# Which engine copies which turn of the probabilities: even turns to ScalarE and odd ones to VectorE, exponents dealt behind turns 0 and 4, batch 8 loaded in two parts (Flamingo block, two layers, one core)

## The chip, the core and the metric

The kernel runs on one core of a Trainium2 chip. The metric is the device time in microseconds (us) of a whole execution; lower is better. Engines are called as in the profile: PE (TensorE), PEld (its weight loads), DVE (VectorE), ACT (ScalarE), POOL (GpSimd), SP (SyncE). Besides times of several runs there is one execution recorded by the hardware profiler, whose rows are called the trace here.

## The reference

Two gated layers on a residual stream x of 8 batches of 100 rows of 512. Each layer is a cross attention over a context of 722 rows (16 heads of 32) and then a feed-forward network. Layer 0 masks the context and its network is ternary; layer 1 has an output projection and a network with quantised activations and weights.

```python
# x (8, 100, 512), ctx (8, 722, 512), mask (8, 722), 16 heads of 32
x = x + tanh(g_xattn[0]) * xattn0(layernorm(x), ctx, ctx, mask)
x = x + tanh(g_ffn[0])   * ffn0(layernorm(x))
x = x + tanh(g_xattn[1]) * xattn1(layernorm(x), ctx, ctx)
x = x + tanh(g_ffn[1])   * ffn1(layernorm(x))

def xattn(x_q, x_k, x_v):               # q, k, v: projections with biases, split into heads
    scores = einsum('bhqw,bhkw->bhqk', q, k) / sqrt(32)
    scores = scores - 10000.0 * (1.0 - mask)      # layer 0 alone
    p = softmax(scores, axis=-1)
    h = einsum('bhqk,bhkw->bhqw', p, v)
    return h                            # layer 1: h @ Wo.T + bo
```

## The kernel before, in words

Everything is one stream of instructions, whose order is written out by hand: each engine runs its instructions in the order in which the program issues them, and waits on semaphores where it needs another engine's result. The program holds the whole computation twice, and the second copy runs only where a test of the inputs asks for it; in the runs here one copy runs.

`attention` goes through 8 batches b and, in each, 4 groups oc of 4 heads. One group is: `scores` of the first half of the keys (L387: 4 matmuls, L395; DVE adds the bias and takes the maximum, L404), a loop of 5 steps, `scores` of the second half, `exponents` started with `negm` (L418, DVE, the negated row maximum), `between`, and `settle`. What is settled is the group before, so probabilities are turned one group after their scores. The four exponents of a group (`next(exps)`, L421, ACT, 0.90 us each) are issued during the `settle` of the group before it and, what is left of them, in the loop of the next group.

`settle` (L506) has six turns, c = 0 to 5, called t0 to t5 here. A `turn` (L430) is 4 transposes of 120 or so keys into a PSUM bank (L436) and one copy of that bank to SBUF, by DVE (L439) or by ACT (L441); `vector` is true wherever both take part: in layer 0 and for b = 0 to 6 of layer 1. For b = 7 of layer 1 ACT copies all of them. The tag `pst` has two banks, so the transposes of t2 need the copy of t0 to be done, t3 that of t1, and so on; other tiles use the same two banks (`ps_xn` of the layernorm, the rows of `finish`, the quantised rows). After each turn follow, in this order: `take(0.74)`, which issues so many us of fill; an exponent, if c is in `dealt`; and a step of `state["spare"]`. Fill is the next batch's projections of keys and values (`projections`, L263): matmuls into one of two other banks and their evictions (layer 0: kT by ACT L321, v by DVE L341 and L342; layer 1, in three passes: kT by ACT L285 and then DVE L288, v by ACT L301 and then DVE L302). After the six turns `values` (L444) multiplies all six copies, in the order of the turns, by v (L448) into a part of the bank of t4, and DVE copies the result (L455).

Around this stand other pieces of DVE work, in the order of the program. `finish` (L457) closes a batch; its chain is issued during oc = 0 and oc = 1 of the next batch (layer 0: L468 to L498 and L135; layer 1: L481, L487, L496, L498, L135). `between0` issues, for oc = 1 in layer 0, `mask_bias` of the next batch (three DVE operations on 100x722, L991, L993, L994), ahead of the settle's turns; for (b, oc) = (6, 3) it starts `normalised`, a layernorm (L142 to L163), and for later groups splits of it (L584, L585). `between1` sets `state["spare"]` to the quantisation of token rows (L820 to L845, with `ln_rstd`, L155 to L159, and L163) for some groups with oc = 0 and oc = 2 of b = 4 to 7.

The context is loaded in parts by `PARTS`: in layer 0 two of 384 and 338 columns, in layer 1 three of 242, 240 and 240. Layer 1 works with a three-pass split (`make_split`), but its first batch, called batch 8 here, is projected during layer 0's last batch by the plain `make`: for each part, 4 x 4 matmuls into `ps_k` (L313) and 4 evictions to kT. `load_ctx(B, 2)` in `follow0` (L1025) loads its third part.

Of the kernel before, what the change touches and what calls it, by code (L numbers as in the profile page):

```python
# [9 lines left out]
F32 = mybir.dt.float32  # L10
F32R = mybir.dt.float32r
# [11 lines left out]
B, S, D = 8, 100, 512  # L23
# [3 lines left out]
P = 128  # L27
KC = D // P
# [2 lines left out]
HALF = SK // 2  # L31
NK = 6

PARTS = ([(0, 384), (384, 338)], [(0, 242), (242, 240), (482, 240)])
KEYS = (
    [(c * P, min(P, SK - c * P)) for c in range(NK)],
    [(0, 122)] + [(122 + c * 120, 120) for c in range(NK - 1)],
# [16 lines left out]
def flow(tc: tile.TileContext, a: dict, out: bass.AP, verdict):  # L54
# [23 lines left out]
    rooms = {}  # L78
# [37 lines left out]
    def take(us):  # L116
        state["owed"] += us * state["pace"]
        while state["owed"] > 0:
            spent = next(state["fill"], None)
            if spent is None:  # L120
                state["owed"] = 0.0
                return
            state["owed"] -= spent
# [64 lines left out]
    def load_ctx(i, part):  # L188
        k0, kn = PARTS[i // B][part]
        t = rooms["ctx"].tile([P, KC, PARTS[0][0][1]], F32, tag="ctxT", name=f"ctxT{i}_{part}")  # L190
        nc.sync.dma_start(t[:, :, :kn], a["ctxT"][i % B][:, :, k0 : k0 + kn])
        ctx_tiles[i, part] = t

    def split_ctx(i, part, idle=False):


        k0, kn = PARTS[1][part]
        sets = [
            rooms["ctx"].tile([P, KC, PARTS[1][0][1]], F32R, tag=t, name=t, bufs=2)
            for t in ("ctx_h", "ctx_l", "ctx_d")  # L200
        ]
        engine = nc.vector if idle else nc.gpsimd
        for half in range(2):
            cs = slice(half * KC // 2, (half + 1) * KC // 2)
            raw = rooms["ctx"].tile([P, KC // 2, PARTS[1][0][1]], F32, tag="ctx_raw", name="ctx_raw")
            nc.sync.dma_start(raw[:, :, :kn], a["ctxT"][i % B][:, cs, k0 : k0 + kn])
            xh, xl, xd = (t[:, cs, :kn] for t in sets)
            if idle:
                nc.scalar.activation(xh, raw[:, :, :kn], AF.Copy, scale=HIGH)
            else:  # L210
                nc.gpsimd.tensor_scalar_mul(xh, raw[:, :, :kn], HIGH)  # L211
            engine.tensor_sub(xl, raw[:, :, :kn], xh.bitcast(F32))
            if idle:
                nc.scalar.activation(xl, xl.bitcast(F32), AF.Copy, scale=LEAP)
            else:
                nc.gpsimd.tensor_scalar_mul(xl, xl.bitcast(F32), LEAP)
            engine.tensor_sub(xd, xh.bitcast(F32), xl.bitcast(F32))
        ctx_tiles[i, part] = sets
# [27 lines left out]
    def three_passes(ps, n, xs, ws, key_cols, out_cols, keys_move):  # L246


        for col, which in ((0, (0, 1)), (256, (2,))):
            for c in range(KC):  # L250
                for k in which:
                    x, w = xs[k][:, c, key_cols], ws[k][:, c, out_cols]
                    nc.tensor.matmul(  # L253
                        ps[:, col : col + n],
                        w if keys_move else x,
                        x if keys_move else w,
                        start=(c == 0 and k == which[0]),
                        stop=(c == KC - 1 and k == which[-1]),
                    )
                    if (col, c) != (256, KC - 1):  # L260
                        yield n / 2400 + 0.016

    def projections(i, wk, wv, bk, more):  # L263
# [3 lines left out]
        layer = i // B  # L267
# [3 lines left out]
            load_ctx(i + 1, 0)  # L271

        def make_split():
            for part, (k0, kn) in enumerate(PARTS[1]):
                xs = ctx_tiles.pop((i, part))
                if part < 2:
                    split_ctx(i, part + 1)
                elif more:
                    split_ctx(i + 1, 0)
                for oc in range(KC):  # L280
                    ps = ps_p.tile([P, 512], F32, tag="ps", name="ps_k")
                    rows_of = slice(oc * P, (oc + 1) * P)
                    yield from three_passes(ps, kn, xs, wk, slice(0, kn), rows_of, True)
                    dst = kT[:, oc, k0 : k0 + kn]
                    nc.scalar.activation(  # L285
                        dst, ps[:, :kn], AF.Identity, scale=1.0 + 1.0 / LEAP, bias=bk[:, oc : oc + 1]
                    )
                    nc.vector.scalar_tensor_tensor(  # L288
                        dst, ps[:, 256 : 256 + kn], -1.0 / LEAP, dst, ALU.mult, ALU.add
                    )  # L290
                    yield kn / 2400 + 0.016
                for half in range(2):
                    cols = slice(half * 256, (half + 1) * 256)
                    for kc, (r0, rn) in enumerate(KEYS[1]):
                        if not k0 <= r0 < k0 + kn:
                            continue
                        ps = ps_p.tile([P, 512], F32, tag="ps", name="ps_v")
                        keys = slice(r0 - k0, r0 - k0 + rn)
                        yield from three_passes(ps[:rn], 256, xs, wv, keys, cols, False)
                        dst = v[half][:rn, kc, :]  # L300
                        nc.scalar.activation(dst, ps[:rn, :256], AF.Copy, scale=1.0 + 1.0 / LEAP)  # L301
                        nc.vector.scalar_tensor_tensor(  # L302
                            dst, ps[:rn, 256:], -1.0 / LEAP, dst, ALU.mult, ALU.add
                        )
                        yield 256 / 2400 + 0.016
# [77 lines left out]
    def attention(layer, kv, follow, qT, bias_of, between, wo, bv, bo, pick):  # L383
# [46 lines left out]
        def turn(ps, c, vector):  # L430

            k0, kn = KEYS[layer][c]
            bank = ps_t.tile([P, 512], F32, tag="pst", name="ps_pT")
            pt = bank[:, : 4 * S].rearrange("p (j s) -> p j s", j=4)
            for j in range(4):
                nc.tensor.transpose(pt[:kn, j, :], ps[j][:, k0 : k0 + kn], ident[:S, :S])  # L436
            sb = rooms["pT"].tile([P, 4, S], F32, tag="pT", name="pT", bufs=6)
            if vector and c % 2 == 0:
                nc.vector.tensor_copy(sb[:kn], pt[:kn])  # L439
            else:  # L440
                nc.scalar.copy(sb[:kn], pt[:kn])  # L441
            return sb, bank[:, 4 * S : 5 * S]

        def values(oc, v, pT, o, oT):  # L444
            for c, (k0, kn) in enumerate(KEYS[layer]):
                for j in range(4):
                    cols = slice((4 * oc % 8 + j) * W, (4 * oc % 8 + j + 1) * W)
                    nc.tensor.matmul(  # L448
                        o[j * W : (j + 1) * W, :],
                        v[oc // 2][:kn, c, cols],  # L450
                        pT[c][:kn, j, :],
                        start=(c == 0),
                        stop=(c == NK - 1),
                    )
            nc.vector.tensor_copy(oT[:, oc, :], o)  # L455
# [50 lines left out]
        def settle():  # L506
            b0, oc0, v0, ps0, oT0, sums0 = held
            vector = layer == 0 or b0 < B - 1
            dealt = (1, 4) if layer and 0 < b0 < B - 1 else (0, 2, 4)
            got = []  # L510
            for c in range(NK):
                got.append(turn(ps0, c, vector))
                take(0.74)
                if c in dealt:
                    next(exps, None)
                next(state["spare"], None)
            values(oc0, v0, [g[0] for g in got], got[NK - 2][1], oT0)
            if oc0 < KC - 1:
                return iter(())
            end = finish(b0, oT0, sums0)  # L520
            next(end)
            return end
# [38 lines left out]
        def last():  # L561
            for _ in exps:
                yield
            take(1.5)
            for _ in settle():
                yield
# [455 lines left out]
    def follow0(b):  # L1022
        if b + 1 < B:
            return projections(b + 1, wk, wv, bk, True)
        load_ctx(B, 2)  # L1025
        later["kv"] = projections(B, wk1, later["wv"], bk1, False)
        return later["kv"]

# [2 lines left out]
    def between0(b, oc):  # L1031
# [8 lines left out]
        if (b, oc) >= (B - 2, KC - 1):  # L1040
            later["xs"] = next(entering)

    ending = attention(0, kv, follow0, qT, lambda b: biases[b], between0, None, bv, None, None)
    for _ in inspected:
        pass
# [286 lines left out]
```

## Time and profile before

| what | value |
|---|---|
| median of 3 runs | 1822.77 us (1818.52 to 1824.11) |
| profiled execution | 1816.73 us, its span 1814.8 us |
| mean granted clock of TensorE | 0.976 |
| layer 0's attention, about | 45 to 605 us |
| layer 0's network, about | 605 to 1165 us |
| layer 1's attention, about | 1215 to 1627 us, its last batch and the rows' network to the end |

Times in the trace are us from the start of the span. In the groups of the page the number behind the bar is busy time and the mean of one instruction in ns, and behind the second bar the idle time of the engine just before them, with the releaser that ended most of it. In the list of waits the numbers are us in total, times, and the longest. A line of the timeline has the start, the duration, the engine, the source line, the operation with its tiles, how many of them, and in brackets the idle time before it and what ended that.

### The profile page before, as it was taken

How to read it: one execution, taken by the hardware profiler on the slowest of the kernel's cores; microseconds unless marked ns; L12 is line 12 of the kernel's file. 1: busy time of each engine (PE TensorE's matmuls, PEld its weight loads, DVE VectorE, ACT ScalarE, POOL GpSimd, SP SyncE). 2: the span in 40 equal slices, each digit the busy share in tenths (PEclk: the TensorE clock that was granted, in tenths of full speed). 3: DMA queues.
4: the chain of work that ended last, by engine and by line, in shares of the span. 5: the costliest groups of instructions: out<-in, count | busy, mean ns of one | idle time of the engine just before them, and what ended most of it. 6: DMA issues, size and time to landing. Idle time of an engine off the chain costs nothing. (4 is left out here: it accounts for less than half of the span.)

```text
span 1814.8 us, 30628 instructions
## 1 busy us (share of the span) xinstructions
PE 1698.7 (94%) x12491; PEld 1308.2 (72%) x12491; DVE 871.9 (48%) x2412; ACT 641.9 (35%) x1349; POOL 666.6 (37%) x543
## 2 busy tenths in 40 slices
PE   8999999999989999999989999899999999998876
PEld 4555555555555899999988999878888877874443
DVE  2545555545555421145451011445555666767764
ACT  1133333333334444422231111234444544453431
POOL 0798998882030000010000000224555444513222
PEclk9999999999999999999999999999999999999888
DMA  7345444451130368778674555410011000110000
GB/s 205 121 146 160 142 156 152 142 167 40 29 117 1 119 222 291 263 251 301 225 231 141 183 186 181 148 45 24 23 28 29 23 23 24 29 71 5 6 10 21
DMA packets 64332, 212.33 MB, mean 117 GB/s; under 512 B 7426, under 2 KB 30978, under 8 KB 51822
## 3 DMA queue, kind: packets, MB, share of 16 engines
q0 software_dynamic: 25344, 138.42, 23.5%
q1 hardware_dynamic: 38838, 71.86, 13.0%
q8 instruction: 100, 1.64, 0.4%
q14 instruction: 50, 0.41, 0.1%
HBM read 205.48 MB, written 4.78 MB: 116 GB/s over the span
## 5 line engine op out<-in xcount | busy, mean ns | idle before, releaser
L604 PE MATMUL ps_h<-hi,h 128*128 128x400 f32 x1024 | 359.4, 351 | 0.0
L604 PE MATMUL ps_h<-lo,h 128*128 128x400 f32 x1024 | 357.1, 349 | 0.0
L421 ACT ACTIVATE p<-p,negm 100x722 f32<-100x722 f32 x256 | 229.3, 897 | 117.9 <-DVE negm L418 117.6
L436 PEld LDWEIGHTS ps_pT<-ident,p 100*128 100x128 f32 (+3 forms) x1536 | 164.9, 139 | 118.3 <-issue 41.0
L436 PE MATMUL ps_pT<-ident,p 100*128 100x100 f32 (+3 forms) x1536 | 199.6, 253 | 32.0 <-DVE pT L439 17.3
L333 PE MATMUL ps_v<-wv,ctxT 128*128 128x512 f32 (+3 forms) x432 | 217.9, 615 | 0.0
L313 PE MATMUL ps_k<-ctxT,wk 128*128 128x384 f32 (+3 forms) x608 | 204.1, 465 | 8.7 <-DMA ctxT<-in_ctxT 8.7
L731 POOL TENSOR_TENSOR seen<-seen,part 128x1024 int32<-128x1024 int32 x88 | 209.2, 2377 | 7.5
L585 DVE TENSOR_TENSOR lo<-g,hi 128x400 fp32r<-128x400 f32 x96 | 55.2, 575 | 305.9 <-ACT hi L584 305.9
L604 PEld LDWEIGHTS ps_h<-lo,h 128*128 128x128 f32 x1024 | 195.7, 191 | 0.5
L604 PEld LDWEIGHTS ps_h<-hi,h 128*128 128x128 f32 x1024 | 195.7, 191 | 0.5
L579 POOL DMA_DIRECT2D h<-in_h_w x64 | 34.7, 541 | 376.5 <-PE ps_h L604 368.6
L439 DVE COPY pT<-ps_pT 128x400 f32<-128x400 f32 (+1 forms) x180 | 102.9, 571 | 114.7 <-PE ps_pT L436 113.7
L313 PEld LDWEIGHTS ps_k<-ctxT,wk 128*128 128x128 f32 x608 | 107.2, 192 | 63.5 <-issue 29.0
L404 DVE CUSTOM_DVE_ANT_0 p<-sc,mask 100x361 f32<-100x361 f32 x256 | 121.3, 531 | 62.0 <-PE sc L395 61.6
L441 ACT COPY pT<-ps_pT 120x400 f32<-120x400 f32 (+3 forms) x204 | 99.6, 490 | 101.7 <-PE ps_pT L436 99.6
L211 POOL TENSOR_SCALAR ctx_h<-ctx_raw 128x480 fp32r<-128x480 f32 (+1 forms) x40 | 56.7, 1417 | 214.5 <-PE ps_v L253 164.0
L404 DVE CUSTOM_DVE_ANT_0 p<-sc,zero 100x361 f32<-100x361 f32 x256 | 121.7, 531 | 24.8 <-PE sc L395 24.4
L659 ACT ACTIVATE g<-ps_h,h_s 128x400 f32<-128x400 f32 x64 | 38.1, 596 | 243.5 <-PE ps_h L604 243.5
L333 PEld LDWEIGHTS ps_v<-wv,ctxT 128*128 128x128 f32 (+3 forms) x432 | 70.7, 187 | 54.6 <-issue 52.9
L321 ACT ACTIVATE kT<-ps_k,bk 128x384 f32<-128x384 f32 (+3 forms) x76 | 41.6, 547 | 181.9 <-PE ps_k L313 181.1
L730 POOL CAST part<-w_seen 128x1024 int32<-128x1024 uint16 x88 | 92.4, 1050 | 27.2 <-DMA w_seen<-in_h_w 17.9
(199 smaller groups left out, 3028.1 us busy)
## 6 DMA issues: line engine op xcount, KB each, us to landing
h<-in_h_w POOLq DMA_DIRECT2D x64, 1024.0 KB, 5.3
w_seen<-in_h_w POOLq DMA_DIRECT2D x64, 512.0 KB, 4.1
w<-in_w POOLq DMA_DIRECT2D x16, 1024.0 KB, 5.3
w_seen<-in_w POOLq DMA_DIRECT2D x16, 512.0 KB, 4.1
w_gate<-in_w_gate SPq DMA_DIRECT2D x16, 512.0 KB
w_up<-in_w_up SPq DMA_DIRECT2D x16, 512.0 KB
w_down<-in_w_down SPq DMA_DIRECT2D x16, 512.0 KB
w<-in_w_w POOLq DMA_DIRECT2D x8, 1024.0 KB, 6.4
```

Of the source, the lines that this page charges most:

```text
L211: nc.gpsimd.tensor_scalar_mul(xh, raw[:, :, :kn], HIGH)
L313: nc.tensor.matmul(ps[:, :kn], wk[:, c, oc * P : (oc + 1) * P], cT[:, c, :kn], start=(c == 0), stop=(c == KC - 1),)
L333: nc.tensor.matmul(ps[:rn, :], cT[:, c, r0 - k0 : r0 - k0 + rn], wv[:, c, :], start=(c == 0), stop=(c == KC - 1),)
L404: nc.vector.tensor_tensor_reduce(ps[j][:, cols], sc[j][:S, :HALF], bias[:, cols], 1.0, LOWEST, ALU.add, ALU.max, m2[:, j, h : h + 1],)
L421: nc.scalar.activation(ps[j], ps[j], AF.Exp, bias=negm[:, j : j + 1], accum_out=sums[:, 4 * oc + j : 4 * oc + j + 1],)
L436: nc.tensor.transpose(pt[:kn, j, :], ps[j][:, k0 : k0 + kn], ident[:S, :S])
L439: nc.vector.tensor_copy(sb[:kn], pt[:kn])
L441: nc.scalar.copy(sb[:kn], pt[:kn])
L585: nc.vector.tensor_sub(two[1][:, cols], src, two[0][:, cols].bitcast(F32))
L604: nc.tensor.matmul(acc[:, :TH], w[:, c, :], part, start=(c == 0 and k == 0), stop=(c == len(ins) - 1 and k == len(two) - 1),)
L730: nc.gpsimd.tensor_copy(part, low)
L731: nc.gpsimd.tensor_tensor(seen, seen, part, ALU.add)
```

## The change

1. In `turn`, where `vector` holds, ACT copies t0, t2 and t4 and DVE copies t1, t3 and t5; before it was the other way round.
2. In `settle`, exponents are dealt behind t0 and t4 wherever `vector` holds. Before, layer 1 with 0 < b0 < 7 dealt them behind t1 and t4, and all the rest behind t0, t2 and t4; b0 = 7 of layer 1 stays so. The exponents not dealt are issued in the loop of the next group.
3. Batch 8 is loaded and projected in two parts, of 362 and 360 columns; the splits of batches 9 to 15 keep their three parts under the new name `SPLIT_PARTS`, and `load_ctx(B, 2)` goes.

```diff
-PARTS = ([(0, 384), (384, 338)], [(0, 242), (242, 240), (482, 240)])
+PARTS = ([(0, 384), (384, 338)], [(0, 362), (362, 360)])
+SPLIT_PARTS = [(0, 242), (242, 240), (482, 240)]
...
     def split_ctx(i, part, idle=False):
-        k0, kn = PARTS[1][part]
+        k0, kn = SPLIT_PARTS[part]
...
         def make_split():
-            for part, (k0, kn) in enumerate(PARTS[1]):
+            for part, (k0, kn) in enumerate(SPLIT_PARTS):
...
         def turn(ps, c, vector):
...
-            if vector and c % 2 == 0:
+            if vector and c % 2:
                 nc.vector.tensor_copy(sb[:kn], pt[:kn])
             else:
                 nc.scalar.copy(sb[:kn], pt[:kn])
...
         def settle():
...
             vector = layer == 0 or b0 < B - 1
-            dealt = (1, 4) if layer and 0 < b0 < B - 1 else (0, 2, 4)
+            dealt = (0, 4) if vector else (0, 2, 4)
...
     def follow0(b):
         if b + 1 < B:
             return projections(b + 1, wk, wv, bk, True)
-        load_ctx(B, 2)
         later["kv"] = projections(B, wk1, later["wv"], bk1, False)
```

Lines are those of the kernel before; in the changed kernel they are one higher from `split_ctx` on.

More of the change, by code (lines that the diff above doesn't have):

```diff
@@ L194, in split_ctx @@
     def split_ctx(i, part, idle=False):
-        k0, kn = PARTS[1][part]
+        k0, kn = SPLIT_PARTS[part]
         sets = [
-            rooms["ctx"].tile([P, KC, PARTS[1][0][1]], F32R, tag=t, name=t, bufs=2)
+            rooms["ctx"].tile([P, KC, SPLIT_PARTS[0][1]], F32R, tag=t, name=t, bufs=2)
             for t in ("ctx_h", "ctx_l", "ctx_d")
@@ L204, in split_ctx @@
             cs = slice(half * KC // 2, (half + 1) * KC // 2)
-            raw = rooms["ctx"].tile([P, KC // 2, PARTS[1][0][1]], F32, tag="ctx_raw", name="ctx_raw")
+            raw = rooms["ctx"].tile([P, KC // 2, SPLIT_PARTS[0][1]], F32, tag="ctx_raw", name="ctx_raw")
             nc.sync.dma_start(raw[:, :, :kn], a["ctxT"][i % B][:, cs, k0 : k0 + kn])
```

## The prediction

> **What bounds the kernel now.** The page first. TensorE (PE) is busy 1698.7 of 1814.8 us, and only 32.0 us of its idle time stand before the transposes of the probabilities, the step that this change touches:
>
> ```profile
> PE 1698.7 (94%) x12491; PEld 1308.2 (72%) x12491; DVE 871.9 (48%) x2412; ACT 641.9 (35%) x1349; POOL 666.6 (37%) x543
> ...
> L436 PE MATMUL ps_pT<-ident,p 100*128 100x100 f32 (+3 forms) x1536 | 199.6, 253 | 32.0 <-DVE pT L439 17.3
> ...
> L439 DVE COPY pT<-ps_pT 128x400 f32<-128x400 f32 (+1 forms) x180 | 102.9, 571 | 114.7 <-PE ps_pT L436 113.7
> ```
>
> DVE and ACT have room; a copy costs about the same on both (571 and 490 ns), so the change can win only by when a copy is done. The waits of PE say which copies are late:
>
> ```profile
> PE ps_pT L436 <- DVE pT L439: 17.3, 14, 5.4
> PE ps_pT L436 <- ACT pT L441: 11.2, 9, 2.6
> ...
> PE ps_pT L448 <- ACT pT L441: 2.3, 6, 0.4
> PE ps_pT L448 <- DVE pT L439: 2.2, 5, 1.2
> ```
>
> That is 33 us, the pool from which it is paid. Third, the timeline at these waits, which have two places. In layer 1, groups with oc = 1:
>
> ```profile
> 1280.57 0.13 DVE L418 TENSOR_REDUCE negm<-m 100x4 f32<-100x8 f32 x1
> 1280.61 0.56 DVE L439 COPY pT<-ps_pT 122x400 f32<-122x400 f32 x1
> 1280.73 0.90 ACT L421 ACTIVATE p<-p,negm 100x722 f32<-100x722 f32 x1 [0.61 <-DVE negm L418]
> ...
> 1281.23 0.56 PE L436 MATMUL ps_pT<-ident,p 100*120 100x100 f32 x4 [1.00 <-DVE pT L439]
> ```
>
> The chain of `finish` has kept DVE until 1280.6; turn 0's copy (call turns t0 to t5) comes behind it and `negm`; t2 needs t0's bank and waits 1.00. In layer 0, oc = 1, `mask_bias` stands ahead of the copies instead:
>
> ```profile
> 295.64 0.47 ACT L441 COPY pT<-ps_pT 128x400 f32<-128x400 f32 x1
> 296.17 0.57 PE L436 MATMUL ps_pT<-ident,p 100*128 100x100 f32 x4 [1.80 <-ACT pT L441]
> 296.26 1.63 DVE L994 TENSOR_SCALAR mask<-mask,mask_m 100x722 f32<-100x722 f32 x1
> 297.81 0.56 DVE L439 COPY pT<-ps_pT 128x400 f32<-128x400 f32 x1
> 298.43 0.56 PE L436 MATMUL ps_pT<-ident,p 100*128 100x100 f32 x4 [0.81 <-DVE pT L439]
> ```
>
> t1 was copied first, by ACT, but behind an exponent that waits for `negm`; t2 took its bank and t3 that of t0. Last, the granted clock by windows behind two such waits (PE column, then the clock, third from the end):
>
> ```profile
> 165.80:169.20 3.40, 3.36 (x11) 2.22 (x12) 1.13 (x3) 1.38 (x3) 3.32 (x3) 0.52 0.48 154
> 298.40:301.80 3.40, 3.37 (x18) 2.00 (x18) 1.70 (x4) 1.64 (x4) 3.31 (x3) 1.00 0.46 154
> ```
>
> After PE waited 1.93 us it ran at 0.52 for some 3.4 us, which costs 1.7; after 1.80 it did not.
>
> **Part 1, the copies, layer 0.** After the change t0 goes to ACT at once, ahead of the first exponent, so t2 starts on time; t1's copy takes on DVE the place that t0's had, and t3 waits for it. What counts is when t3 starts.
> - b = 1, 3, 4 (before: waits of .55 + 1.93, 1.80 + .81, 2.37 + .82): t3 starts at the same moment as now. Gain 0. The two waits become one of 2.4 to 3.2 us. At b = 1 and 4 the clock fell already; at b = 3 it did not, and by the rows (1.93, 2.37 and 2.58 dropped it) it will: -1.7.
> - b = 2: t2's wait of 2.58 ended at 230.81 and its fill ran at half clock, so that t3 began at 233.28; DVE's copy ends at 231.85. Gain 1.0 to 1.4, taken 1.0.
> - b = 0: wait .36 goes; t3 would start at 96.0, DVE's copy ends at 95.07. Gain .36. b = 5, 6: t2's .43 goes, t3 then waits some .2: gain .2 each.
> - b = 6, oc = 3, where `normalised` holds DVE: one wait of 5.38 until 525.74. t2 and its fill (1.2 us) now run inside the wait. Gain 1.2 to 1.9, taken 1.5.
> - Three waits of 1.1 on L585 concern t1's bank, which another tile holds: unchanged.
> Sum 0.4 + 1.0 + 0.4 + 1.5 - 1.7 = 1.6; bounds -0.5 (t3's copy a little late everywhere) and 4.5 (no drop, the larger ends).
> [...]
>
> **Part 1, layer 1, b < 7.**
> - oc = 1, b = 1 to 6: waits of t2 of 1.00 (three) and 1.15 (three), 6.45 in all. After: DVE's copy, now of t1, ends at 1281.17, and t3, with t2 on time at 1280.23, is due at 1281.2. t4 needs t2's copy on ACT, behind an exponent: 1280.73 + .90 + .49 = 1282.1, due 1282.2. The later three leave .15 each: gain 6.0.
> - oc = 3, b = 1 to 6: `values` stops .39 each time in its last part, since t5's copy on ACT stands behind the exponent dealt behind turn 4:
>
> ```profile
> 1312.64 0.90 ACT L421 ACTIVATE p<-p,negm 100x722 f32<-100x722 f32 x1
> 1313.52 0.48 ACT L441 COPY pT<-ps_pT 120x400 f32<-120x400 f32 x1
> 1314.05 0.38 PE L448 MATMUL ps_pT<-pT,v 120*32 120x100 f32 x8 [0.39 <-ACT pT L441]
> ```
>
> t5's copy is now DVE's, behind L302 (1312.78 + .42), done by 1313.8 where 1313.66 would be on time: .1 to .15 stays. Of 2.34, 1.4 to 2.3 gained, taken 1.8.
> - Groups with token rows on DVE (oc = 2 of b = 4, 5, 6): t0's copy escapes the chain L155 to L163, t1's does not (it moves from ACT to behind L155 to L159, .67 mean to .88, .16, .16, .25), so that t3 waits, and t5's lands behind L836 or L839. Each 0.4 to 0.6 worse, taken 1.5 for the three.
> - b = 0, oc = 3: .67 + .32 stay but for .1. Settle of (6,3), during b = 7: the 1.16 before `values` on t4 at 1646.17 is put off to t5, whose matmuls start 1.0 later, but t3 waits in between: 0 to 1, taken .4.
> Sum 6.0 + 1.8 - 1.5 + .1 + .4 = 6.8; bounds 4 and 8.5.
>
> **Part 2, the exponents.** Layer 0 (and b = 0 of layer 1): the one behind turn 2 goes to the next group's loop, so ACT has two there instead of one; layer 1: one moves from behind turn 1 to turn 0. Two take 2 x .90 us of a loop of over 6, and the turns that read them come a loop later; the kT evictions (L321, .58) that may queue behind them have a second bank and four matmuls (2.8 us) of slack. Cost nothing; without that cover .9 a group, which no row shows. Behind turn 0 or 1 the exponent waits for `negm` alike, and no copy of t0 waits behind it any more.
>
> **Part 3, batch 8.** 48 matmuls of 240 columns become 32 of 360. In the timeline of L313 one of 240 takes .45 us, of 338 .61, of 384 .69; so .65 for 360: 48 x .45 - 32 x .65 = 0.8 us on PE, which is the bound there (562 to 592). Bounds 0 and 1.5. Four evictions and one load fewer were hidden; SP issues one DMA less ahead of the scales.
>
> **Sum.** 1.6 + 6.8 + 0.8 = 9.2 us of the profiled execution's 1816.73: 0.51%. That execution lies 0.33% under the median 1822.77; the same share of the median gives 1813.5.
>
> **Rivals.**
> - *No clock drop at b = 3*: 1.7 better, 1811.8. For: the 1.80 there dropped nothing, and neither did three waits of 1.1.
> - *The wait only moves*: in oc = 1 of layer 1, t3 waits for t1's DVE copy as t2 did for t0's, as in layer 0. The 6.0 go and 3.2 stay: 1819.6, within 0.3% (5.5 us, about what a measurement here can tell from no change). For: the copy ends at 1281.17 against a due time of 1281.2, no slack at all. Against: a .1 late costs only .1.
> - *Slower: t5 on DVE comes last.* DVE evicts values in pairs (L302 with L288, .42 + .41; L341 with L342, pitch .33), and each settle's last copy now stands behind them and right before `values`, which reads it 1.07 us after it begins. With .57 for the copy, .5 is spare; from a DVE backlog over .5 us on, each of some 46 settles that have no wait at their end now loses .4 (one eviction): 46 x .4 = 18.4, less 9.2, is 9.2 slower, 1832. For: the page has DVE 50 to 70% busy in the slices of layer 1. Against: t4's copy had to be done sooner, and for it `values` waited only 5 times, 2.2 us.
>
> **How the numbers follow.** Forecast (with the drop) .58, without it .12: together faster by over 0.3%, .70. Moved wait, or half of it with the token rows worse: same, .16. Slower: .14, .12 of it the third rival. The terms' bounds give 3.5 to 14.5 us, 1808 to 1819; the moved wait reaches 1819.6, part of the third rival 1824, and the before's runs spread from 1818.5 to 1824.1, so the range is 1806 to 1824.
>
> **What would show it.** The waits of L436 on DVE and ACT together fall from 28.5 to some 20, on DVE alone hardly in layer 0 (its rows stand at t3 now), in layer 1 from 8.0 to under 3; L448 on ACT loses its six of .39, L448 on DVE grows a little. L313 has 16 x 2 records fewer. The window behind 298.4 shows a clock near .5. Wrong: L448 waits on DVE in most settles (third rival), t3 waits near 1.0 in oc = 1 of layer 1 (second), or waits of `ps_k` on L321 in layer 0.

## The result, and the profile after

The changed kernel took 1815.5 us in the median of 10 runs (1808.93 to 1816.88), the kernel before 1823.44 in 10 (1816.96 to 1828.67): a ratio of 0.9963, 95% interval 0.9946 to 0.9980. Measured again later beside other kernels, it had 0.9980 (0.996 to 1.000; 12 runs). So it is faster by 0.2 to 0.4%, 4 to 7 us; forecast were 9.2 us, 0.51%.

The two profiled executions do not show this gain: 1816.86 us after, near the slowest run of its ten, against 1816.73 before, below the fastest of its ten. Totals of single traces are therefore not compared below; stages are, over several traces. Page of the changed kernel:

```profile
PE 1701.9 (94%) x12459; PEld 1302.0 (72%) x12459; DVE 875.5 (48%) x2412; ACT 641.0 (35%) x1345; POOL 666.1 (37%) x543
...
L437 PE MATMUL ps_pT<-ident,p 100*128 100x100 f32 (+3 forms) x1536 | 199.6, 253 | 31.9 <-DVE pT L440 24.0
```

The idle time of PE before the turns' transposes is what it was, 31.9 against 32.0 us. Its releasers have changed, as the list of waits of PE shows (us in total, times, longest):

```profile
PE ps_pT L437 <- DVE pT L440: 24.0, 16, 4.8
...
PE ps_pT L437 <- DVE xc L586: 4.5, 4, 1.4
PE ps_pT L437 <- ACT pT L442: 3.0, 3, 1.2
...
PE ps_pT L449 <- DVE pT L440: 1.7, 3, 0.8
```

The 11.2 us on ACT's copies fell to 3.0 (those of b = 7), and DVE's rose from 17.3 to 24.0. By windows the two layers part. Layer 1, 1240 to 1629 us, the kernel before and then the changed one:

```profile
PE ps_pT L436 <- DVE pT L439: 8.0, 9, 1.1
PE ps_pT L448 <- ACT pT L441: 2.3, 6, 0.4
PE ps_pT L448 <- DVE pT L439: 1.1, 4, 0.3
```

```profile
PE ps_pT L437 <- DVE pT L440: 4.3, 8, 0.8
PE ps_pT L449 <- DVE pT L440: 1.6, 2, 0.8
```

11.4 us became 5.9. In layer 0, from 110 to 495 us, 11.7 us (ACT 8.16, DVE 3.56) became 14.3, all of it at t3:

```profile
PE ps_pT L437 <- DVE pT L440: 14.3, 6, 4.3
```

This holds beyond the one pair: the three traces with the old copies, the mask in its place and POOL at work (before, l1_only, deal_and_parts below) have 11.7 to 13.4 us here, the three with the new ones (after, after_again, l0_and_parts) 14.0 to 14.4.

### The profile page after: what moved, and what is told of

The parts are those of the page before. It is cut to its first block, busy times and chain, and to the rows that moved or that the text cites. A ratio compares the mean times of both kernels' runs of the same rounds, so it can differ in the third digit from the quotient of the medians.

```text
span 1815.0 us, 30479 instructions
## 1 busy us (share of the span) xinstructions
PE 1701.9 (94%) x12459; PEld 1302.0 (72%) x12459; DVE 875.5 (48%) x2412; ACT 641.0 (35%) x1345; POOL 666.1 (37%) x543
## 5 line engine op out<-in xcount | busy, mean ns | idle before, releaser
L437 PE MATMUL ps_pT<-ident,p 100*128 100x100 f32 (+3 forms) x1536 | 199.6, 253 | 31.9 <-DVE pT L440 24.0
L732 POOL TENSOR_TENSOR seen<-seen,part 128x1024 int32<-128x1024 int32 x88 | 209.6, 2382 | 7.5
L442 ACT COPY pT<-ps_pT 128x400 f32<-128x400 f32 (+2 forms) x204 | 99.8, 491 | 241.7 <-PE ps_pT L437 241.5
L314 PEld LDWEIGHTS ps_k<-ctxT,wk 128*128 128x128 f32 x576 | 100.8, 192 | 66.3 <-issue 28.8
L731 POOL CAST part<-w_seen 128x1024 int32<-128x1024 uint16 x88 | 92.0, 1046 | 21.6 <-DMA w_seen<-in_h_w 14.4
```

The source lines that it names most:

```text
L314: nc.tensor.matmul(ps[:, :kn], wk[:, c, oc * P : (oc + 1) * P], cT[:, c, :kn], start=(c == 0), stop=(c == KC - 1),)
L731: nc.gpsimd.tensor_copy(part, low)
L732: nc.gpsimd.tensor_tensor(seen, seen, part, ALU.add)
```

## The experiments

Stages over all the traces, in us: *layer 0* is from the first turn to the first matmul of its network, *layer 1* from its first split matmul to the first matmul of the token rows (L871). "Old" and "new" are the parity of the copies in that layer.

| kernel | layer 0 | layer 1 | ratio to before |
|---|---|---|---|
| before | 513.1 old | 459.1 old | |
| after | 518.5 new | 455.8 new | 0.9963 |
| after_again | 514.2 new | 456.6 new | 0.9980 |
| l1_only | 517.5 old | 455.2 new | 0.9980 (0.9964 to 0.9995) |
| l0_and_parts | 518.9 new | 459.6 old | 1.0024 (1.0003 to 1.0045) |
| deal_and_parts | 517.3 old | 459.5 old | 1.0008 (0.9989 to 1.0028) |
| quiet_before | 490.6 old | 459.1 old | 0.9884 (0.9863 to 0.9906) |
| quiet_after | 489.0 new | 455.0 new | 0.9855 (0.9833 to 0.9878) |
| mask_before | 506.6 old | 459.8 old | 0.9946 (0.9929 to 0.9962) |
| mask_after | 500.2 new | 455.4 new | 0.9899 (0.9874 to 0.9925) |
| mask_after_2 | 500.4 new | 455.1 new | 0.9871 (0.9849 to 0.9893) |

**Halves of the change.** For layer 0 there were two theories: "phase", that its loss is POOL's doing and differs from execution to execution, and "own loss", that one merged wait is dearer than two in itself. So layer 1 was changed alone, and then all but layer 1:

```diff
 l1_only, from before
-            if vector and c % 2 == 0:
+            if vector and c % 2 == (1 if layer else 0):
-            dealt = (1, 4) if layer and 0 < b0 < B - 1 else (0, 2, 4)
+            dealt = (0, 4) if layer and b0 < B - 1 else (0, 2, 4)
 l0_and_parts, from after
-            if vector and c % 2:
+            if vector and c % 2 == (0 if layer else 1):
-            dealt = (0, 4) if vector else (0, 2, 4)
+            dealt = (1, 4) if layer and 0 < b0 < B - 1 else (0, 2, 4) if layer else (0, 4)
```

> The change in layer 1 only: parity and dealt exponents of layer 1, layer 0 and batch 8 as before. Both theories: layer 1 between its start and L872's first wait near 1629 is 4.1 us shorter, of which b = 7 gives 0.8 back, so 3 us faster (ratio 0.998). If the whole measured gain of 7 to 8 us were layer 1's, 0.9957 here.

> The change without layer 1: parity and dealt exponents changed in layer 0 only, batch 8 in two parts. Theory 'phase': 2 to 5 us faster than before (ratio 0.997 to 0.999), and its profile may end layer 0 on either side of 605. Theory 'own loss': 3 to 5 us slower (1.002 to 1.003) with waits of L436 near 14 us between 110 and 495 again.

l1_only gave 0.9980, 3.6 us, as expected. l0_and_parts was 4.4 us slower, as "own loss" had it; but its layer 0 (518.9) is only 1.4 longer than that of l1_only (517.5), whose layer 0 is the one of before. The halves do not add to the whole, which was run again:

> The changed kernel once more, beside the next three. The halves measured +0.24% (layer 0 with batch 8) and -0.20% (layer 1), which add to 0, but the whole measured -0.37%. Theory 'halves add': the layer 0 half costs 2 to 4 us while POOL inspects weights, so here 0.998 to 1.002. Theory 'whole': the first measurement stands, 0.995 to 0.998, and the half of layer 0 was dear only in its company (three-turn exponents in b = 0 of layer 1, or its draw of runs).

Again 0.9980; its interval up to 1.000 takes in both theories in part. What holds over the traces is that layer 1 gains 3.9 (mean of five old 459.4, of six new 455.5), and that layer 0, while POOL inspects weights and the mask is where it was, is 513.1 to 517.5 old and 514.2 to 518.9 new: no gain, with a scatter of some 4 us in one and the same code.

That scatter can be taken apart. PE's waits in layer 0 are 23.0 to 25.0 us in the three old traces and 25.2 to 26.3 in the three new; the halved clock cost it 10.2 to 13.7 and 8.5 to 13.7 (an estimate: half of the halved time). What is left when both are taken off is 478.6 to 481.6 us in all fourteen traces of this document. So the new parity waits 1 to 2 us longer here, and one stretch of halved clock more or less (3.41 us, by that estimate 1.7 us lost) hides that.

**Where the scatter comes from.** The ternary weights are inspected by POOL during layer 0's attention (L721 to L731). This was cut to the first block, so both kernels leave the rest of the inspection out:

```diff
-        blocks = [src[:, h * n : (h + 1) * n] for src in blocks for h in range(2)]
+        blocks = [src[:, h * n : (h + 1) * n] for src in blocks for h in range(2)][:1]
```

> The kernel before, with only the first block of ternary weights inspected instead of all of them, so that POOL is nearly idle in layer 0's attention (the inspection of the other blocks is left out). Measured for comparison with the next run. Theory 'phase': in layer 0 the time of DVE's finish and mask chains depends on how they fall against POOL's additions (L731), so here L994 takes 0.6 us and L498 0.75 us each time, the stall list of oc = 1 shrinks to under 1 us each, layer 0's attention ends 10 us or more before 605.3, and the five times lie within 3 us of each other (before: 11 us). Theory 'own loss': POOL has no part in it; layer 0 ends within 3 us of 605.3 and the scatter stays.

> The changed kernel with the same inspection left out. Theory 'phase': the 5.1 us by which layer 0's attention ended later in the changed kernel's profiled execution were POOL's; against quiet_before, layer 0 (with batch 8) ends 1 to 3 us earlier, layer 1 up to 1629 gains its 4.1 us, and the total is 4 to 7 us lower. Theory 'own loss': merging t2's and t3's waits makes each mask group slower by itself; layer 0 ends 3 to 5 us later than in quiet_before and the total is within 2 us of it.

In quiet_before layer 0 is 23 to 27 us shorter than in the three old traces; 14 to 16 us of that are waits of PE and 8.5 to 12 the halved clock, and the mask groups wait .43 each, at t2. The edit leaves out the loads of these weights too, and no run here parts them from POOL's work. The same groups of DVE instructions from 110 to 495 us (busy us, mean ns), first after with POOL at work, then quiet_after:

```profile
L499 DVE SCALAR_TENSOR_TENSOR x<-t,tg,x 100x512 f32<-100x512 f32 x6 | 10.0, 1659 | 0.2
L476 DVE TENSOR_TENSOR t<-t,brow 100x512 f32<-100x512 f32 x6 | 9.0, 1494 | 0.2
L994 DVE TENSOR_REDUCE mask_m<-mask 100x1 f32<-100x722 f32 x6 | 5.4, 905 | 0.2
```

```profile
L994 DVE TENSOR_REDUCE mask_m<-mask 100x1 f32<-100x722 f32 x6 | 5.4, 905 | 0.2
L499 DVE SCALAR_TENSOR_TENSOR x<-t,tg,x 100x512 f32<-100x512 f32 x6 | 4.5, 752 | 0.2
L476 DVE TENSOR_TENSOR t<-t,brow 100x512 f32<-100x512 f32 x6 | 4.2, 692 | 0.2
```

L499 and L476 stretch 2.2 times beside POOL, the mask's L995 1.6 times (597 to 939 ns); the reduction (905 ns) does not. The clearest row is L157 of `normalised` in the kernel before: it works on 100x4, starts at 521.18 and ends at 523.38, and one of POOL's additions (L731) runs from 521.01 to 523.35; in quiet_before L157 takes .17, and the wait of 5.38 at (6,3) is .87. From 110 to 495 us of the changed kernel each row of L476 and L499 of 1.40 us or more (seven of twelve, up to 2.77) and each of L995 of 1.62 (two of six) has an addition of POOL (L732) beside it, and where none is beside them they take .69, .75 and .60; not every addition stretches them (L476 took .69 from 358.58, beside one from 358.60), and the reduction takes .90 to .91 with one and without. Why some are stretched and others not, no run shows. So by these rows how long the chain of `finish` and the mask hold DVE depends on how POOL's additions fall. "Phase" was right on this cause, and wrong that quiet runs lie within 3 us: they spread over 11 (1792.59 to 1803.92), so there is scatter elsewhere. Without POOL the pair differs by 4.0 us in the medians, with overlapping intervals: layer 0 gains 1.6, layer 1 4.2 by the stages.

**The mask out of the way.** In both kernels its three DVE operations become spare steps behind turns 1, 3 and 5:

```diff
-            biases[b + 1] = mask_bias(b + 1)
+            state["spare"] = mask_bias(b + 1)
+            next(state["spare"])
 def mask_bias(b):  # a generator now, with biases[b] = mf
         nc.sync.dma_start(mi, a["mask"][b : b + 1, :].partition_broadcast(S))
+        yield
+        yield
         nc.vector.tensor_copy(mf, mi)
+        yield
+        yield
...
         nc.vector.reduce_max(mm, mf, axis=AX.X)
+        yield
+        yield
         nc.vector.tensor_scalar(mf, mf, mm, MASK_C, ALU.subtract, ALU.mult)
```

> The changed kernel with the three DVE operations of the next batch's mask bias dealt behind turns 1, 3 and 5 of the oc = 1 settle of layer 0, instead of all ahead of turn 0. The order of work is the only difference. If the merged waits at t3 (4.2, 4.3, 3.0, 2.3 us) come from the mask operations ahead of t1's copy, they fall to about 1 us each and the time by 8 to 12 us against after_again. If DVE is late there already through the finish chain (L476, L499 stretched by POOL), only 2 to 4 us go, and the waits stay near 2 to 3 us.

> The kernel before with the same dealing of the mask bias. With t0's copy on DVE ahead of the mask operations and t1's on ACT, the waits of .55 + 1.93, 2.58, 1.80 + .81, 2.37 + .82 should fall to about .5 each, 6 to 10 us less than before. Against mask_after it shows what the parity of layer 0 is worth once the mask is out of the way: forecast 3 to 5 us in favour of the changed kernel, nearly all of it layer 1's.

mask_after: 1800.05 us, 16 below after_again and more than the 8 to 12 expected; its waits in the window of layer 0 are 4.6 where they were 14.3, and with them most halved stretches went: in layer 0 the clock cost 3.4 us, by the same estimate, where it cost 8.5 in after_again:

```profile
PE ps_pT L437 <- DVE pT L440: 4.6, 6, 1.4
```

mask_before: 1811.05, 10 below before. With the mask gone from its front, the new parity is worth 6.4 us in layer 0 (500.2 against the 506.6 of the one trace of mask_before; the medians of the runs are 11.0 apart, of which layer 1 has some 4), four times what it is with POOL quiet: t1 comes one turn later than t0, and now that turn counts: DVE is held by `finish` alone, t2 waits 2.24, 2.26, 1.38 and 1.34 for t0's copy in mask_before, and t3 at most 1.36 for t1's in mask_after.

**The dealing by itself.**

```diff
 deal_and_parts, from before, with PARTS as in the change
-            dealt = (1, 4) if layer and 0 < b0 < B - 1 else (0, 2, 4)
+            dealt = (0, 4) if vector else (0, 2, 4)
```

> The kernel before with its old parity, but the exponents dealt behind turns 0 and 4 and batch 8 in two parts. By the prediction moving exponents costs nothing and batch 8 gains .8 us: the ratio within 0.9985 to 1.0005, and the waits of layer 1 (t2 in oc = 1, the last part of values in oc = 3) as in the kernel before. If the dealing itself were what frees layer 1, its six waits of 1.0 to 1.15 or its six of .39 would be gone.

Ratio 1.0008, a little above what was expected, its interval holding 1. Layer 1's waits stayed, 1240 to 1629 us:

```profile
PE ps_pT L437 <- DVE pT L440: 7.4, 8, 1.1
PE ps_pT L449 <- ACT pT L442: 1.9, 5, 0.4
```

(This stage ends at 1634.4, so its sixth wait of .39, at 1632.65, lies behind the window.)
The dealing by itself frees nothing; in layer 1 it takes the parity of the copies (the new parity with the old dealing was not run).

**What stands ahead of t1's copy.** After, layer 1, oc = 1 of b = 1:

```profile
1285.05 0.13 DVE L419 TENSOR_REDUCE negm<-m 100x4 f32<-100x8 f32 x1
1285.09 0.40 DVE L289 SCALAR_TENSOR_TENSOR kT<-ps_k,kT 128x240 f32<-128x240 f32 x1
1285.41 0.56 DVE L440 COPY pT<-ps_pT 120x400 f32<-120x400 f32 x1
1286.03 0.56 PE L437 MATMUL ps_pT<-ident,p 100*120 100x100 f32 x4 [0.38 <-DVE pT L440]
```

In the kernel before `negm` was followed by t0's copy, and L288 came behind it. t1 is issued one `take` later, and that fill's eviction now stands ahead. To take it away, t0 and t1 were issued back to back:

```diff
 pair_after, from after
                 got.append(turn(ps0, c, vector))
-                take(0.74)
+                if c or not vector:
+                    take(1.48 if vector and c == 1 else 0.74)
                 if c in dealt:
                     next(exps, None)
-                next(state["spare"], None)
+                if c or not vector:
+                    next(state["spare"], None)
```

> The changed kernel with turns 0 and 1 issued back to back where both engines copy: the fill and the spare step that stood between them come after turn 1 (fill of 1.48 instead of .74 + .74). Theory 'one more turn of evictions': t1's DVE copy waits because one turn's fill (L289, or L342 and L343, or the chain L156 to L160) is issued ahead of it. Then the oc = 1 waits of layer 1 (.38, .38, .38, .52, .53, .52) fall under .2, the .81 and .80 at t3 of the token-row groups go, the wait of 4.84 near 529 falls by .7, and the time is 3 to 5 us below after. Rival: DVE is simply late through its finish chain and negm; the waits at t3 stay within .1 and the time within 1 us of after.

> Turns 0 and 1 back to back and the mask bias dealt behind turns 1, 3 and 5, together on the changed kernel. If the two edits are independent, mask_after's 0.990 and some 3 us more: 0.987 to 0.990. If the mask operations were what the pair gains from in layer 0, no better than mask_after.

A miss: 1.0025 (1.0011 to 1.0039), 8 to 11 us above the changed kernel, by its two ratios, instead of 3 to 5 below it, and pair_mask 0.9953, worse than mask_after alone. The waits named did go, but others came, in layer 1 and, second fence, in layer 0 from 535 to 612 us (4.5 there in the changed kernel):

```profile
PE ps_pT L437 <- DVE t L497: 3.4, 6, 0.6
```

```profile
PE ps_pT L437 <- DVE xc L588: 7.9, 4, 2.0
```

t1 takes a bank that `finish` (L497), the split of the layernorm (L588) or the token rows (L859, 1.1 us in five waits) used last, and the fill between t0 and t1 had covered that. The waits listed for layer 1 are 8.4 us, 2.5 more than in the changed kernel, and the stage is 4.3 longer (460.1); the other 1.8 are left open.

**A better version.** The spare step behind turn 0 alone is left out, and the fill between the turns stays:

```diff
 mask_spare1, from mask_after, with one yield less at the start of mask_bias
-                next(state["spare"], None)
+                if c or not vector:
+                    next(state["spare"], None)
```

> mask_after, with the spare step behind turn 0 left out where both engines copy (every spare step comes one turn later), so that t1's DVE copy stands ahead of the chain L156 to L160 in the token-row groups of layer 1; the fill between t0 and t1 stays. If that chain is what holds t3 there, the waits of .79 and .80 at t3 go, those of .77 at the last part of values shrink or stay, and the time is 1 to 2.5 us below mask_after. If it only moves, as the back-to-back turns did, the same time within 1 us and a wait at another turn.

> mask_after once more, beside mask_spare1: 0.988 to 0.992 of before, waits in oc = 1 of layer 0 between 0 and 1.4 us again, whatever POOL's phase, since only negm and not the mask operations stands ahead of t1's copy.

mask_spare1 is the fastest: 1795.44 us, 0.9835 (0.9811 to 0.9860) beside 0.9871 for mask_after_2, so 5 us in the medians with intervals that overlap a little. Of the token-row waits .82 and .80 at t3 and .76 and .78 at `values` are gone; the oc = 1 waits of b = 4 to 6 rose from .52 to .96. Layer 1 is 454.3 against 455.1, so the trace accounts for 0.8 of the 5.

## Why the prediction was right, and where its steps were off

**Direction and range held**; the gain of 4 to 7 us is 0.4 to 0.8 of the forecast. Its place was right for layer 1, and wrong for layer 0 and batch 8. That the first measurement lies within 2.0 us of the forecast 1813.5 is partly the luck of its draw, since the stages show a gain in layer 1 alone. Of the signs, the six waits of .39 went as said, but the waits of the transposes for DVE's and ACT's copies fell from 28.5 us together to 27.0 only, where some 20 was forecast.

**Layer 1: forecast 6.8, measured 3.9 to L871 and .4 to .9 behind it.** Wait by wait:
- oc = 1: 6.0 forecast, 3.7 measured: .38 (three times) and .52 (three) stay at t3. The step that failed: "DVE's copy, now of t1, ends at 1281.17", that is, t1's copy inherits t0's place. It is issued one turn later, behind one eviction more (L289, .40).
- oc = 3: 1.8 forecast, all 2.34 gained.
- b = 0: .1 forecast, .99 gained; that t2's copy, for which t4 waited, is no longer DVE's was not followed through.
- Token rows: -1.5 forecast, 1.62 of waits became 3.18, -1.56.
- Settle of (6,3): +.4 forecast. The wait of 1.16 became .16. From L871's wait near 1629 to the scores near 1650 it took 19.89 before and 20.66 after, but that pair misleads: behind the same three waits of PE (.61, .21, 1.11) the clock halved after and not before. Where it halved, the stretch takes 21.1 to 21.5 in four old traces and 20.66 in five new ones; where it did not, 19.89 old and 19.02 new (mask_after_2). So .4 to .9 is gained, and this term held.

Of the 5.5 us of waits that went, 3.9 show in the stage; the halved clock cost it 5.1 us in the mean on both sides, by the same estimate, so it does not explain the rest, which was not found.

**Layer 0: forecast 1.6, measured none or a loss.** "t3 starts at the same moment" held as a mechanism: t3 is released by t1's copy behind the mask. The gains at b = 2 and others were read from one execution, and POOL's phase moves them by more than their size (b = 2 waited 4.29 after, 2.94 in after_again). In (6,3), 1.5 was forecast; the wait went from 5.38 to 4.84 only. Before, t0's copy came right behind L163 (523.62 + 1.58, the copy at 525.12); now L342 and L343 (527.98 and 528.32) stand between L164 and t1's copy at 528.65: .67 lost, again to the evictions of one fill more. The three waits on the layernorm's split, put down as unchanged (3.4 us), became four with 4.3 to 4.6; in deal_and_parts, with the old copies, they are 3.9.

**The clock drop at b = 3** (-1.7) did not come in this execution, where the wait was 2.97; in after_again, the same code, the wait was 4.17 and it came. Windows behind the 2.97 and behind the wait of 4.24 at b = 1, in the changed kernel:

```profile
303.60:307.00 3.40, 3.34 (x18) 2.01 (x18) 1.52 (x5) 1.45 (x4) 3.31 (x4) 1.00 0.31 116
167.10:170.50 3.40, 3.37 (x11) 2.24 (x12) 1.21 (x3) 0.00 (x0) 3.32 (x3) 0.50 0.48 154
```

So 1.93 us dropped the clock before, with another wait close ahead of it, and 2.97 did not here. In these rows the length of one wait is no threshold. By these traces it matters how a wait falls on a grid: in each of the fourteen traces the halved stretches start whole steps of 3.413 us apart and last one, two or three steps. From 60 to 605 us all 49 drops from the full clock follow a step in which PE was busy for at most .48 of it, and only two such steps (.45 and .47) were followed by the full clock. (The ends of matmuls, and so these shares, are modelled.) Of the wait of 1.93 us 1.75 fell into one step, of the 4.17 us 3.29; the 2.97 us were cut into 1.51 and 1.46. Steps of the kernel before, of the changed kernel and of after_again (PE busy is the second number, the clock the third from the end):

```profile
162.25:165.66 3.41, 1.45 (x6) 0.62 (x6) 3.34 (x4) 1.05 (x3) 3.32 (x4) 1.00 0.39 131
165.66:169.07 3.41, 3.23 (x11) 2.09 (x12) 1.27 (x4) 1.38 (x3) 3.33 (x3) 0.50 0.48 154
```

```profile
298.78:302.20 3.42, 1.92 (x8) 0.70 (x6) 3.35 (x12) 1.05 (x3) 3.42 (x3) 1.00 0.37 125
302.20:305.61 3.41, 1.95 (x11) 1.32 (x12) 2.60 (x6) 0.37 (x2) 3.33 (x3) 1.00 0.53 154
```

```profile
293.00:296.41 3.41, 0.12 (x1) 0.12 (x2) 3.34 (x5) 0.98 (x3) 3.41 (x3) 1.00 0.31 112
296.41:299.83 3.42, 3.42 (x11) 2.19 (x12) 1.06 (x3) 0.18 (x1) 3.34 (x3) 0.50 0.40 153
```

**Batch 8: forecast 0.8, measured 0.** From t2 of the last mask group (489.14 before) to layer 0's network it takes 116.1 us before and 116.2 in l1_only, with three parts, and 116.4 in deal_and_parts, with two. The term that was mis-sized is the cost of a matmul: in the traces it has two records, which start .204 us apart with 240 columns and .304 with 360 at full clock, so 48 x .41 less 32 x .61 is .2 us and not .8, and the waits on the layernorm's split, .45 longer with two parts, take more than that.

**Exponents: forecast nothing**, and deal_and_parts shows nothing. **The slower rival** (t5 on DVE late in every settle) did not appear: `values` waits for DVE 3 times, 1.7 us. **The moved wait** came in part, .38 to .53 where 1.0 would have made it "same".

## What to carry to other kernels

When alternating work changes sides, the first item of a slow engine does not take over the old first item's place in its queue: whatever is issued between the two items, evictions above all, now stands ahead of it (here L289, .40 us). Look first at what holds that engine when the first item comes; here moving the mask's three operations behind the copies brought 16 us (10 with the old copies) where swapping the copies brought 4 to 7. And a wait that a second engine stretches (4.29 and 2.94 us at b = 2 in two traces of one code), or one behind which the clock may halve (it did behind 4.17 us at b = 3, and not behind 2.97, in the same two), has to be read from several executions before it is priced.

## What the runs showed of the hardware that was not expected

- Without POOL's inspection and its loads layer 0's attention was 23 to 27 us shorter (quiet_before against the three old traces). Beside the inspection DVE operations of .69 to .75 us take 1.5 to 1.7 in the mean and 2.8 at worst (L476 and L499 in the changed kernel), and one on 100x4 takes 2.20 instead of .17 (L157 in the kernel before and in quiet_before).
- The clock stayed at 1.00 behind waits of 2.25 and 2.97 us, and fell to 0.50 with 4.24 and 4.29; in the fourteen traces it halves on a grid of 3.413 us, for whole steps, and the same waits in the same code (.61, .21 and 1.11, behind layer 1's stage in mask_after and mask_after_2) dropped it in one trace and not in the other.
